# Ternary feed-forward with gathered conditioning on one core: another order for the first block

## The chip, the cores and the metric

The kernel runs on one core of a Trainium2 chip. The metric is the device time of one execution in microseconds (us), the median of three runs: 972.67 us before the change (972.66 to 973.07).

## The reference

```python
w = weights[conditions]                        # 128 samples, each a 64 x 64 matrix out of 200
u = einsum('bct,bcd->bdt', x, w)               # x: 128 x 64 x 512
# ternarize(W): delta = 0.05 * max|W|; mask = |W| > delta
#               alpha = sum(|W| where mask) / max(sum(mask), 1); Wq = alpha * sign(W) * mask
h = gelu(u @ ternarize(W1).T + b1)             # W1: 2048 x 512
y = h @ ternarize(W2).T + b2                   # W2: 512 x 2048
scale = max|y| / 7 + 1e-8
out = x + clip(round(y / scale), -7, 7) * scale
```

So each weight matrix needs its largest magnitude, then a count of the weights above the threshold and the sum of their magnitudes, before its factor alpha is known. Layer 1 may be multiplied with the plain signs before alpha is there; GELU needs alpha.

## The kernel before, in words

**Blocks.** The 128 samples go in 16 blocks of 8 (four pairs of samples, 512 columns). For each block the rows of x are mixed by the gathered matrices ("pc" products), split into a high and a low part, run through 16 chunks of layer 1 ("ph") and 16 chunks of layer 2 ("py"). Blocks 1 to 15 run in a steady order in which the two layers are interleaved two chunks apart (lines 963 to 1133). Block 0 is different, and the change lies almost wholly in it.

**Order of the work.** Every engine runs its instructions in program order: `InOrder` (line 28) wraps each engine, and line 36 is the line that all instructions carry in the profile, so groups are told apart by tile names. What each engine does next is what the Python program says next for it.

**Block 0, in order of time.**
- SP loads W1 in seven pieces, x of block 0 in two halves, b1 and W2 (lines 113 to 137). DVE takes the largest magnitudes of W1, ACT its signs and magnitudes (lines 283 to 296). PE meanwhile runs 50 products of ones ("idle", line 281) into a bank that nobody reads.
- POOL gathers four 128 x 64 tables (`fetch`, line 174, one indirect DMA for each pair) and writes each, times 64, in two 64 x 64 pieces on the diagonal of `diag` (`place`, line 186).
- The threshold: DVE's row maxima go through a transposition on PE (`thresholds`, line 229; "tops_delta_w" in the profile), then four pairs are mixed on PE (`mix0`, line 303).
- DVE makes masks (`mask1`, 128 x 2048 for each of four groups of W1) and ternary weights (`signed1`, "terns"). POOL widens one 128 x 512 chunk of them at a time to 32 bits (`widen1`, "wf<-terns", into a ring of four). A layer-1 chunk is four products with the widened weights and the high part of the mixed x, and four with the narrow weights and the low part (`layer1_0`, line 416).
- PE counts the masks (`count1`, line 339): the stationary operand is ones, a 128 x 256 piece of the mask moves, 32 products in all, into one bank "number". `alpha_1` (line 535) reduces the 256 columns on DVE; ACT sums the magnitudes (`above1`).
- Layer-1 chunks before alpha is known wait in PSUM banks (`early`, line 517, five banks in turn). `early_bend` (line 528) is then the GELU on ACT, a rounded copy on ACT, and the difference of the two: on POOL for chunks 0, 2, 4 and 6 ("h<-ring,h"), later on DVE for the others (`low`, line 468).
- DVE finds the maxima of W2 (`largest2`), its threshold (a second transposition on PE, "tops_delta_w<-ident_f,junk"), and its ternary weights (`signed2`: a comparison of 128 x 2048, "junk<-nat,minus_w", then a second instruction, "terns<-nat,delta_w,junk").
- POOL widens W2's chunks (`widen2`, a ring of four) and PE runs layer 2 of block 0 with them (lines 698 to 722); both the high and the low part of a chunk are multiplied with the widened weights. Between its chunks block 1 is mixed (`condition`, from layer-2 chunk 5 on), with tables that POOL fetched and placed at lines 613 to 638.

**Numbers that set the order:** `widen1` runs two chunks ahead of `early` (line 682); `behind(hc)` (line 662) says what DVE, ACT and POOL do after layer-1 chunk hc.

Of the kernel before, what the change touches and what calls it, by code (L numbers as in the profile page):

```python
# [8 lines left out]
F32 = mybir.dt.float32  # L9
# [7 lines left out]
ALU = mybir.AluOpType  # L17
# [3 lines left out]
P = 128  # L21
# [3 lines left out]
UP = 64.0  # L25
# [14 lines left out]
def tile_cond_ternary_ffn(  # L40
# [32 lines left out]

    const = ctx.enter_context(tc.tile_pool(name="const", bufs=1))
    big = ctx.enter_context(tc.tile_pool(name="big", bufs=20))
    gather = ctx.enter_context(tc.tile_pool(name="gather", bufs=PAIRS))
    half = ctx.enter_context(tc.tile_pool(name="half", bufs=8))
    quarter = ctx.enter_context(tc.tile_pool(name="quarter", bufs=4))
    ps_c = ctx.enter_context(tc.tile_pool(name="ps_c", bufs=2, space=PSUM))
# [84 lines left out]
    def half_of(h):  # L164
        return slice(h * C, (h + 1) * C)
# [8 lines left out]
    def fetch(n, j):  # L174

        pair = n * PAIRS + j
        wg = gather.tile([P, D], F32, tag="wg", name=f"wg_{pair}")
        pool.indirect_dma_start(
            out=wg[:, :],
            out_offset=None,  # L180
            in_=table,
            in_offset=bass.IndirectOffsetOnAxis(ap=rows[:, pair : pair + 1], axis=0),
        )
        return wg

    def place(j, wg):
        for h in range(2):
            out = diag[half_of(h), j, h * D : (h + 1) * D]
            pool.tensor_scalar(out, wg[half_of(h), :], UP, None, ALU.mult)

    def parts(n):
        return [
# [69 lines left out]
    def group1(tiles, g):  # L262
        return tiles[g // 2][:, g % 2, :]

    def sign1(g):
        act.activation(group1(signs, g), flat(nat1[g]), AF.Sign)

    def abs1(g):

        if g == NG - 1:  # L270
            mags.append(big.tile([P, GH, T], F32, tag="big", name="mag"))
        else:
            mags.append(nat1[g])
        act.activation(flat(mags[g]), flat(nat1[g]), AF.Abs)

    mags = []


    idle = ps_h.tile([P, T], F32, tag="ph", name="idle")
    pool.memset(above[:, :T], 1.0)  # L280
    for _ in range(50):
        pe.matmul(out=idle, lhsT=ones_b, rhs=above[:, :T], start=True, stop=True)
    at = 0
    for g in range(NG):
        for ks in PIECES[g]:
# [8 lines left out]
        if g < NG - 1:  # L294
            sign1(g)
            abs1(g)
    fetched = [fetch(0, j) for j in range(PAIRS)]
    for j in range(PAIRS):
        place(j, fetched[j])
    two_next = parts(0)  # L300
    pcs = []

    def mix0(j):
        pc = ps_y.tile([P, NT, P], F32, tag=f"py{j}", name=f"pc_0_{j}")
        mix(pair_of(x_next, j), j, pc)
        pcs.append(pc)

# [28 lines left out]
            ALU.mult,  # L336
        )

    def count1(g, number, first, final):
        n = number.shape[1]  # L340
        for i in range(WCH // n):
            pe.matmul(
                out=number,
                lhsT=ones_b,
                rhs=group1(masks, g)[:, i * n : (i + 1) * n],
                start=(first and i == 0),
                stop=(final and i == WCH // n - 1),
            )

    def above1(g):  # L350
# [62 lines left out]
                    stop=(c == NT - 1 and k == 1),  # L413
                )

    def layer1_0(n, hc, ph, part=slice(0, BLK), between=None):
        g, i = divmod(hc, GH)
        narrow = group1(terns, g)[:, i * T : (i + 1) * T].rearrange("p (c h) -> p c h", c=NT)
        for k in range(2):
            w = narrow if k else wide1[n, hc]  # L420
            for c in range(NT):
                if between is not None and k == 1 and c == NT - 2:
                    between()
                pe.matmul(
                    out=ph,
                    lhsT=w[:, c, :],
                    rhs=cond[n][k][:, c, part],
                    start=(c == 0 and k == 0),
                    stop=(c == NT - 1 and k == 1),
                )  # L430
# [83 lines left out]
    ring = [t[:, i, :] for t in rings for i in range(2)]  # L514
    ring += [quarter.tile([P, BLK], F32, tag="quarter", name=f"ring_{i}") for i in (10, 11)]

    def early(hc, between=None):

        slot = (hc + 1) % 5
        if slot < 2:  # L520
            ph = ps_h.tile([P, BLK], F32, tag="ph", name=f"ph_0_{hc}")
        else:
            ph = ps_y.tile([P, BLK], F32, tag=f"py{slot - 2}", name=f"ph_0_{hc}")
        for part in halves if hc == 0 else [slice(0, BLK)]:
            layer1_0(0, hc, ph[:, part], part, between)
        waiting[hc] = ph
# [8 lines left out]
    def alpha_1():  # L535

        count = const.tile([P, 1], F32, name="count1")
        dve.tensor_reduce(count, number, AX.X, ALU.add)
        dve.tensor_scalar(count, count, 1.0, None, ALU.max)
        dve.reciprocal(count, count)  # L540
        yield
        total = ps_c.tile([P, NG], F32, tag="pc", name="total1")
        pe.matmul(out=total, lhsT=ones_f, rhs=sums1, start=True, stop=True)
        kept = const.tile([P, 1], F32, name="kept1")
        dve.tensor_reduce(kept, total, AX.X, ALU.add)
        alpha[0] = const.tile([P, 1], F32, name="alpha_w1")
        dve.tensor_scalar(alpha[0], kept, count, delta1, ALU.mult, ALU.add)
        alpha[1] = without_up(0)
# [14 lines left out]
    def largest2(g):  # L563
        dve.tensor_reduce(
            top_2[:, g : g + 1], flat(nat2[g]), AX.X, ALU.max, apply_absolute_value=True
        )
# [43 lines left out]

    mask1(0, parts1[0])
    signed1(0, parts1[0])
    fetched += [fetch(1, j) for j in range(2)]
    widen1(0, 0)
    widen1(0, 1)
    fetched += [fetch(1, j) for j in range(2, PAIRS)]
    lo0(0)
    lo0(1)
    hi0(2)
# [9 lines left out]
    abs1(3)  # L629
    for g in range(NG):  # L630
        above1(g)
    number = ps_y.tile([P, T // 2], F32, tag="py3", name="number")
    count1(0, number, True, False)
    mask1(1)
    signed1(1)
    widen1(0, 4)
    for j in range(PAIRS):
        place(j, fetched[PAIRS + j])
    mask1(2)
    mask1(3)  # L640
    signed1(2)
    early(2)
    for g in range(1, NG):
        count1(g, number, False, g == NG - 1)
    find = alpha_1()
    next(find)
    early(3, lambda: next(find, None))
    widen1(0, 5)
    early(4)
    early_bend(0)  # L650
    widen1(0, 6)
    wf2 = half.tile([P, 2, T], F32R, tag="half", name="wf2")
    w2f = [wf2[:, i, :] for i in range(2)]
    w2f += [quarter.tile([P, T], F32R, tag="quarter", name=f"wf2_{i}") for i in (2, 3)]
    find = thresholds("w2", top_2, above.bitcast(F32)[:, :P])


    def ahead(hc):
        if hc == 11:
            next(find)  # L660

    def behind(hc):
        if 5 <= hc < 5 + NG:
            largest2(hc - 5)
        if hc == 7:
            sign1(3)
        if hc == 9:
            signed1(3)
        if hc == 11:
            delta.extend(next(find))  # L670
            signed2(0)
        if hc == 12:
            for i in (1, 3):
                low(0, i)
            signed2(1)
        if hc in (13, 14):
            widen2(0, hc - 13)

    for hc in range(5, NH):
        ahead(hc)  # L680
        early(hc)
        if hc + 2 < NH:
            widen1(0, hc + 2)
        early_bend(hc - 4)
        behind(hc)
    for hc in range(NH - 4, NH):
# [11 lines left out]
    for hc in range(NH - LAG):  # L698
        if hc + 2 < NH - LAG:
            widen2(0, hc + 2)  # L700
        both_layer2(0, hc)
        if hc == 0:
            signed2(2)
        if hc == 1:
            for i in range(10, NH):
                low(0, i)
        if hc < NG:
            kept(w1t, hc, terns)
        if hc == 3:
            signed2(3)  # L710
        if hc == 4:
            two_next = parts(1)
            w2t = big.tile([P, NH, T], F8, tag="big", name="w2t")
        if hc in (4, 6, 8, 9):
            g = {4: 0, 6: 1, 8: 2, 9: 3}[hc]
            count2(g)
            kept(w2t, g, terns2)
        if hc in (5, 7, 9, 11):
            j = (hc - 5) // 2
            condition(1, j, pair_of(x_next, j), two_next)  # L720
            for g in {7: [0], 9: [1], 11: [2, 3]}.get(hc, []):
                sum2(g)
    cond[1] = two_next
    x_next, two_next, fetched = [], [], []
    hf = ring[:2]
    widen1(1, 0)
    widen2(0, NH - LAG)
# [235 lines left out]
    def eight(s):  # L963
# [14 lines left out]
        if n + 1 < NB:  # L978
            if hc == 0:
                if n + 1 == SEVEN[0]:  # L980
                    extra["x"] = half.tile([P, 2, T], F32, tag="half", name="x_quarters")
                    for j in range(2):
                        quarter_x(n + 1, j)
                else:
                    x_next.append(load_x(n + 1) if n + 1 < NB - 1 else split_x(n + 1))
                two_next.append(parts7(n + 1) if n + 1 in SEVEN else parts(n + 1))
            if 2 <= hc < 2 + PAIRS:
                fetched.append(fetch(n + 1, hc - 2))
            if 7 <= hc < 7 + PAIRS:
                place(hc - 7, fetched[hc - 7 - PAIRS])  # L990
        if n == KNOWN and hc in (0, 1):
            fetch_x(order[hc])
        if n == SEVEN[0] - 1:
# [65 lines left out]
    def pair(n, k):  # L1059
# [10 lines left out]
        def behind(i):  # L1070
# [15 lines left out]
            if i == 4:  # L1086
                if not leaves:
                    widen7(ahead, 3)
                if k < PAIRS:
                    fetched.append(fetch(n + 1, k))  # L1090
                if 2 <= k < 2 + PAIRS:
                    place(k - 2, fetched[PAIRS * (n - 1) + k - 2])
                if not leaves:
                    widen7(ahead, 2)
                if parting:
# [147 lines left out]
```

## Time and profile before

| | us |
|---|---|
| median of 3 runs | 972.67 |
| the profiled execution | 972.58 |
| its span (first to last instruction) | 970.8 |
| first layer-1 product of block 0 | 20.32 |
| first layer-1 product of chunk 4 | 31.70 |
| first GELU of block 0 | 32.38 |
| first layer-2 product of block 0 | 53.89 |
| mixing of block 1 for its third pair | 74.08 |
| first layer-1 product of block 1 | 83.30 |

Times inside the execution are counted from the start of the span. PE is matrix products, PEld the loads of their stationary operands, DVE, ACT and POOL the three other compute engines, SP the engine that issues the large DMAs. In a timeline a row is one instruction or a run of like ones: start, duration of the run, engine, operation, output and inputs, shapes, count, and in brackets the idle time before it with what ended it. The records of products overlap, since they are pipelined: how far one start is from the next is what a product costs PE.

### The profile page before, as it was taken

Reading aid. Unit: us, or ns where it says so; the run is one execution under the profiler, and the core shown is the slowest. Engines: PE = TensorE matmul, PEld = TensorE weight load, DVE = VectorE, ACT = ScalarE, POOL = GpSimd, SP = SyncE. Lnnn points to the kernel's source line nnn. Section 1 sums busy time; section 2 is a strip of 40 time slices with the busy share of each in tenths; the row PEclk is TensorE's granted clock in tenths of the full one; section 3 lists DMA queues with packets and bytes.
Section 4 is the critical chain, followed back from the end, with each engine's and each line's share of the span. In section 5 each row is a group of like instructions: output and inputs, shape, how many; then the busy total and the mean of one; then the engine's idle time right before and its main releaser. Section 6 shows DMA issues by size and latency. Waiting matters only on the chain.

```text
span 970.8 us, 16879 instructions
## 1 busy us (share of the span) xinstructions
PE 960.1 (99%) x5858; PEld 727.4 (75%) x5858; DVE 659.7 (68%) x1143; ACT 613.7 (63%) x1076; POOL 662.0 (68%) x1024
## 2 busy tenths in 40 slices
PE   8999999999999999999999999999999999999996
PEld 5677667778788787887887787787887878766664
DVE  7898766666676666666666666666766765467856
ACT  7994445656656566665656666566666666467773
POOL 6877867777676676767677676776767776466541
PEclk9999999999999999999999999999999999999999
DMA  9201011010111100111110111101011111339994
GB/s 358 99 23 47 14 34 49 24 69 15 35 49 34 59 24 35 49 33 48 34 60 15 35 49 33 59 25 55 28 33 51 33 57 48 109 128 371 392 408 180
DMA packets 33158, 80.05 MB, mean 82 GB/s; under 512 B 3760, under 2 KB 3760, under 8 KB 30128
## 3 DMA queue, kind: packets, MB, share of 16 engines
q1 hardware_dynamic: 31024, 76.86, 22.0%
q0 software_dynamic: 2048, 2.10, 0.7%
q8 instruction: 47, 0.77, 0.3%
q14 instruction: 39, 0.32, 0.1%
HBM read 46.44 MB, written 32.51 MB: 81 GB/s over the span
## 4 chain that ended last, share of the span: by engine, by line
PE 97%; DVE 2%; ACT 0%; POOL 0%; issue 0%; ACTq 0%; POOLq 0%
PE py L36 46%; PE xy L36 18%; PE z L36 14%; PE ph L36 11%; PE pc L36 6%; PE idle L36 1%; DVE masks L36 1%; DVE xt L36 0%; DVE y_last L36 0%; DVE terns L36 0%; ACT diag L36 0%; PE number L36 0%; ACT ph L36 0%; DVE ymax L36 0%; DVE low_last L36 0%
## 5 line engine op out<-in xcount | busy, mean ns | idle before, releaser
L36 PE MATMUL py<-wf,h 128*128 128x512 f32 x1056 | 309.7, 418 | 0.0
L36 POOL CAST wf<-w2t 128x512 fp32r<-128x512 fp8e4 x236 | 205.6, 889 | 116.3 <-PE py L36 113.0
L36 DVE SCALAR_TENSOR_TENSOR low_parts<-ring,h 128x512 f16<-128x512 f32 x224 | 188.5, 877 | 85.9 <-ACT h L36 85.7
L36 PE MATMUL py<-w2t,low_parts 128*128 128x512 fp8e4 x944 | 228.0, 379 | 0.0
L36 PEld LDWEIGHTS py<-wf,h 128*128 128x128 f32 x1056 | 192.0, 189 | 44.8
L36 POOL CAST wf<-sums 128x256 fp32r<-128x256 fp8e4 (+1 forms) x288 | 142.1, 498 | 78.3 <-PE xy L36 75.2
L36 ACT ACTIVATE ring<-ring,b1t,alpha_up 128x512 f32<-128x512 f32 x192 | 155.9, 818 | 56.2 <-DVE ring L36 52.0
L36 DVE TENSOR_TENSOR ring<-xy,ring 128x256 f32<-128x256 f32 x192 | 106.6, 555 | 113.2 <-PE xy L36 113.2
L36 ACT COPY ring<-xy 128x256 f32<-128x256 f32 x192 | 71.6, 373 | 176.2 <-PE xy L36 175.0
L36 POOL CAST wf<-w1t 128x256 fp32r<-128x256 fp8e4 (+1 forms) x240 | 140.4, 596 | 27.8 <-PE ph L36 23.4
L36 PEld LDWEIGHTS <-low_parts 128*128 128x128 f16 x944 | 92.1, 98 | 88.8 <-issue 1.7
L36 ACT ACTIVATE h<-ring 128x512 fp32r<-128x512 f32 x224 | 130.3, 627 | 1.1
L36 POOL TENSOR_SCALAR diag<-wg 64x64 f32<-64x64 f32 x128 | 68.0, 532 | 40.0 <-DMA wg<-in_L_cond_weights,rows 36.1
L36 PEld LDWEIGHTS <-w1t 128*128 128x128 fp8e4 x768 | 63.4, 98 | 32.8 <-issue 12.8
L36 PE MATMUL xy<-xb,wf 128*128 128x256 f32 x384 | 84.7, 302 | 0.0
L36 PE MATMUL xy<-xt,wf 128*128 128x256 f32 x384 | 75.4, 277 | 0.0
L36 PE MATMUL xy<-xl,sums 128*128 128x256 f16 x384 | 75.3, 278 | 0.0
L36 POOL DMA_INDIRECT wg<-in_L_cond_weights,rows x64 | 63.0, 985 | 16.5 <-issue 13.7
L36 PE MATMUL xy<-xl,w1t 128*128 128x256 f16 x384 | 74.3, 275 | 0.0
L36 PE MATMUL ph<-x,wf 128*128 128x512 f32 (+1 forms) x260 | 73.2, 403 | 0.1
L36 PE MATMUL z<-xl,sums 128*128 128x256 f16 x384 | 73.2, 273 | 0.0
L36 ACT ACTIVATE ring<-ph,b1t,alpha_up 128x512 f32<-128x512 f32 x48 | 37.3, 777 | 54.7 <-PE ph L36 52.5
(133 smaller groups left out, 1421.8 us busy)
## 6 DMA issues: line engine op xcount, KB each, us to landing
xt<-in_x SPq DMA_DIRECT2D x38, 512.0 KB, 8.3
y_dram<-y SPq DMA_DIRECT2D x15, 1024.0 KB, 4.3
out<-xt SPq DMA_DIRECT2D x30, 512.0 KB, 8.2
x_quarters<-in_x SPq DMA_DIRECT2D x52, 256.0 KB, 2.7
nat<-in_L_ffn_W SPq DMA_DIRECT2D x6, 1024.0 KB, 10.2
y_back<-y_dram SPq DMA_DIRECT2D x2, 1024.0 KB, 10.7
nat<-in_L_ffn_W SPq DMA_DIRECT2D x3, 512.0 KB, 8.9
wg<-in_L_cond_weights,rows POOLq DMA_INDIRECT x64, 2.5
```

Of the source, the lines that this page charges most:

```text
L36: return lambda *args, **kw: self._tc.keep_in_program_order(make(*args, **kw))
```

## The change

Read in order of the file:

- The four gathered tables of a block are one tile, allocated at the first fetch. For blocks 0 and 1 they are placed by `place_all`: two instructions of 64 x (4 x 64) instead of eight of 64 x 64. Later blocks still place pair by pair.
- 46 products of ones instead of 50. The fetches of block 0 stand earlier in the program text; on POOL they are preceded by the same instructions as before.
- The mixed pairs of block 0 lie in other banks, so that layer 1 has six banks instead of five.
- A count product has a 128 x 128 piece of the mask as its stationary operand and one column of ones moving: 64 products instead of 32. The result has one column; a product with ones ("all1") adds it over the partitions, in the middle of chunk 4, where the sums of magnitudes are added too.
- Chunks 2 and 3 of layer 1 both come before the counts of groups 1 to 3; before, only chunk 2 did.
- POOL's order: chunks 0 and 1 are widened before block 1's first two fetches, chunk 5 before its last two, and chunks 6 to 8 before the first difference on POOL; from then on POOL widens three chunks ahead. Block 1's tables are placed after chunk 15 was widened, and no longer between chunks 4 and 5.
- The transposition for W2's threshold is issued in the middle of chunk 11, and no longer before it. Two of DVE's sums over W2 (`sum2`) change places with the mixing.

```diff
+        if j == 0:
+            gathered[n] = gather.tile([P, PAIRS, D], F32, tag="wg", name=f"wg_{n}")
...
+    def place_all(n):
+        for h in range(2):
+            out = diag[half_of(h), :, h * D : (h + 1) * D]
+            pool.tensor_scalar(out, gathered[n][half_of(h)], UP, None, ALU.mult)
...
-    for _ in range(50):
+    for _ in range(46):
         pe.matmul(out=idle, lhsT=ones_b, rhs=above[:, :T], start=True, stop=True)
+    for j in range(PAIRS):
+        fetch(0, j)
...
-    for j in range(PAIRS):
-        place(j, fetched[j])
+    place_all(0)
...
-        pc = ps_y.tile([P, NT, P], F32, tag=f"py{j}", name=f"pc_0_{j}")
+        home, tag = [(ps_c, "pc"), (ps_h, "ph"), (ps_y, "py0"), (ps_y, "py1")][j]
+        pc = home.tile([P, NT, P], F32, tag=tag, name=f"pc_0_{j}")
...
-        n = number.shape[1]
-        for i in range(WCH // n):
+        for i in range(WCH // P):
             pe.matmul(
                 out=number,
-                lhsT=ones_b,
-                rhs=group1(masks, g)[:, i * n : (i + 1) * n],
+                lhsT=group1(masks, g)[:, i * P : (i + 1) * P],
+                rhs=ones_b[:, :1],
...
-        slot = (hc + 1) % 5
+        slot = (hc + 4) % 6
...
-        dve.tensor_reduce(count, number, AX.X, ALU.add)
-        dve.tensor_scalar(count, count, 1.0, None, ALU.max)
+        dve.tensor_copy(count, number)
+        yield
+        all_of = ps_c.tile([P, 1], F32, tag="pc", name="all1")
+        pe.matmul(out=all_of, lhsT=ones_f, rhs=count, start=True, stop=True)
+        dve.tensor_scalar(count, all_of, 1.0, None, ALU.max)
         dve.reciprocal(count, count)
...
-    fetched += [fetch(1, j) for j in range(2)]
     widen1(0, 0)
     widen1(0, 1)
-    fetched += [fetch(1, j) for j in range(2, PAIRS)]
+    for j in range(2):
+        fetch(1, j)
...
-    number = ps_y.tile([P, T // 2], F32, tag="py3", name="number")
-    count1(0, number, True, False)
+    number = ps_c.tile([P, 1], F32, tag="pc", name="number")
+    count1(0)
+    early(2)
     mask1(1)
     signed1(1)
     widen1(0, 4)
-    for j in range(PAIRS):
-        place(j, fetched[PAIRS + j])
+    early(3)
     mask1(2)
     mask1(3)
     signed1(2)
-    early(2)
+    widen1(0, 5)
+    for j in range(2, PAIRS):
+        fetch(1, j)
+    widen1(0, 6)
     for g in range(1, NG):
-        count1(g, number, False, g == NG - 1)
+        count1(g)
     find = alpha_1()
     next(find)
-    early(3, lambda: next(find, None))
-    widen1(0, 5)
-    early(4)
+    early(4, {(1, 0): lambda: next(find), (1, 2): lambda: next(find, None)})
+    widen1(0, 7)
+    early(5)
+    widen1(0, 8)
     early_bend(0)
-    widen1(0, 6)
+    early_bend(1)
...
     def behind(hc):
-        if 5 <= hc < 5 + NG:
+        if hc == 6:
+            largest2(0)
+        if 6 <= hc < 6 + NG - 1:
             largest2(hc - 5)
...
+        if hc == 12:
+            place_all(1)
-        if hc == 9:
+        if hc == 8:
             signed1(3)
...
-    for hc in range(5, NH):
-        ahead(hc)
-        early(hc)
-        if hc + 2 < NH:
-            widen1(0, hc + 2)
+    for hc in range(6, NH):
+        early(hc, {(1, 0): lambda: next(find)} if hc == 11 else {})
+        if hc + 3 < NH:
+            widen1(0, hc + 3)
         early_bend(hc - 4)
         behind(hc)
...
-            for g in {7: [0], 9: [1], 11: [2, 3]}.get(hc, []):
+            for g in {7: [0, 1], 9: [2], 11: [3]}.get(hc, []):
                 sum2(g)
```

More of the change, by code (lines that the diff above doesn't have):

```diff
@@ L75, in tile_cond_ternary_ffn @@
     big = ctx.enter_context(tc.tile_pool(name="big", bufs=20))
-    gather = ctx.enter_context(tc.tile_pool(name="gather", bufs=PAIRS))
+    gather = ctx.enter_context(tc.tile_pool(name="gather", bufs=1))
     half = ctx.enter_context(tc.tile_pool(name="half", bufs=8))
@@ L176, in fetch @@
         pair = n * PAIRS + j
-        wg = gather.tile([P, D], F32, tag="wg", name=f"wg_{pair}")
+        if j == 0:
+            gathered[n] = gather.tile([P, PAIRS, D], F32, tag="wg", name=f"wg_{n}")
         pool.indirect_dma_start(
-            out=wg[:, :],
+            out=gathered[n][:, j, :],
             out_offset=None,
@@ L183, in fetch, with place @@
         )
-        return wg
-    def place(j, wg):
+    def place(n, j):
         for h in range(2):
             out = diag[half_of(h), j, h * D : (h + 1) * D]
-            pool.tensor_scalar(out, wg[half_of(h), :], UP, None, ALU.mult)
+            pool.tensor_scalar(out, gathered[n][half_of(h), j, :], UP, None, ALU.mult)
+    def place_all(n):
+        for h in range(2):
+            out = diag[half_of(h), :, h * D : (h + 1) * D]
+            pool.tensor_scalar(out, gathered[n][half_of(h)], UP, None, ALU.mult)
+    gathered = {}
     def parts(n):
@@ L266, in sign1 @@
         act.activation(group1(signs, g), flat(nat1[g]), AF.Sign)
+    mags = nat1[: NG - 1]
     def abs1(g):
@@ L271, in abs1 @@
             mags.append(big.tile([P, GH, T], F32, tag="big", name="mag"))
-        else:
-            mags.append(nat1[g])
         act.activation(flat(mags[g]), flat(nat1[g]), AF.Abs)
-    mags = []
     idle = ps_h.tile([P, T], F32, tag="ph", name="idle")
     pool.memset(above[:, :T], 1.0)
-    for _ in range(50):
+    for _ in range(46):
         pe.matmul(out=idle, lhsT=ones_b, rhs=above[:, :T], start=True, stop=True)
+    for j in range(PAIRS):
+        fetch(0, j)
     at = 0
@@ L296, in tile_cond_ternary_ffn @@
             abs1(g)
-    fetched = [fetch(0, j) for j in range(PAIRS)]
-    for j in range(PAIRS):
-        place(j, fetched[j])
+    place_all(0)
     two_next = parts(0)
@@ L337, in signed1, with count1 @@
         )
-    def count1(g, number, first, final):
-        n = number.shape[1]
-        for i in range(WCH // n):
+    def count1(g):
+        for i in range(WCH // P):
             pe.matmul(
                 out=number,
-                lhsT=ones_b,
-                rhs=group1(masks, g)[:, i * n : (i + 1) * n],
-                start=(first and i == 0),
-                stop=(final and i == WCH // n - 1),
+                lhsT=group1(masks, g)[:, i * P : (i + 1) * P],
+                rhs=ones_b[:, :1],
+                start=(g == 0 and i == 0),
+                stop=(g == NG - 1 and i == WCH // P - 1),
+                skip_group_check=True,
             )
@@ L414, in layer1, with layer1_0 @@
                 )
-    def layer1_0(n, hc, ph, part=slice(0, BLK), between=None):
+    def layer1_0(n, hc, ph, part=slice(0, BLK), between={}):
         g, i = divmod(hc, GH)
@@ L421, in layer1_0 @@
             for c in range(NT):
-                if between is not None and k == 1 and c == NT - 2:
-                    between()
+                between.get((k, c), lambda: None)()
                 pe.matmul(
@@ L515, in tile_cond_ternary_ffn, with early @@
     ring += [quarter.tile([P, BLK], F32, tag="quarter", name=f"ring_{i}") for i in (10, 11)]
-    def early(hc, between=None):
-        slot = (hc + 1) % 5
+    def early(hc, between={}):
+        slot = (hc + 4) % 6
         if slot < 2:
@@ L655, in tile_cond_ternary_ffn @@
     find = thresholds("w2", top_2, above.bitcast(F32)[:, :P])
-    def ahead(hc):
-        if hc == 11:
-            next(find)
     def behind(hc):
-        if 5 <= hc < 5 + NG:
+        if hc == 6:
+            largest2(0)
+        if 6 <= hc < 6 + NG - 1:
             largest2(hc - 5)
@@ L720, in tile_cond_ternary_ffn @@
             condition(1, j, pair_of(x_next, j), two_next)
-            for g in {7: [0], 9: [1], 11: [2, 3]}.get(hc, []):
+            for g in {7: [0, 1], 9: [2], 11: [3]}.get(hc, []):
                 sum2(g)
     cond[1] = two_next
-    x_next, two_next, fetched = [], [], []
+    x_next, two_next = [], []
     hf = ring[:2]
@@ L987, in eight @@
             if 2 <= hc < 2 + PAIRS:
-                fetched.append(fetch(n + 1, hc - 2))
+                fetch(n + 1, hc - 2)
             if 7 <= hc < 7 + PAIRS:
-                place(hc - 7, fetched[hc - 7 - PAIRS])
+                place(n + 1, hc - 7)
         if n == KNOWN and hc in (0, 1):
@@ L1089, in behind @@
                 if k < PAIRS:
-                    fetched.append(fetch(n + 1, k))
+                    fetch(n + 1, k)
                 if 2 <= k < 2 + PAIRS:
-                    place(k - 2, fetched[PAIRS * (n - 1) + k - 2])
+                    place(n + 1, k - 2)
                 if not leaves:
```

## The prediction

> **What bounds the kernel.** The page first, then the chain of waits, then the timelines of PE, PEld, POOL and DVE for the first 85 us.
>
> ```profile
> span 970.8 us, 16879 instructions
> ...
> PE 97%; DVE 2%; ACT 0%; POOL 0%; issue 0%; ACTq 0%; POOLq 0%
> ```
>
> PE carries 97% of the chain, so what PE saves anywhere reaches the end, unless PE later meets a wait that was hidden. The chain over the first 140 us shows where PE was not the one:
>
> ```profile
> 2.96 13.62 PE idle L36 x50
> 16.58 0.11 PE tops_delta_w L36
> 16.69 3.59 PE pc L36 x32
> ...
> 25.92 3.11 DVE masks L36 x2
> 29.03 0.04 issue
> 29.07 1.03 PE number L36 x8
> 30.10 1.38 PE ph L36 x6
> 31.48 0.12 PE total L36 x2
> 31.60 13.50 PE ph L36 x58
> ```
>
> Until 31.6 PE waits at times for DVE's masks, and the products of ones hold the transposition up; after it, it is PE alone. The counting and the late weights, in PE's and in PEld's timeline:
>
> ```profile
> 24.07 1.04 PE L36 MATMUL number<-masks,ones_b 128*128 128x256 bf16 x8
> 26.80 1.91 PE L36 MATMUL number<-masks,ones_b 128*128 128x256 bf16 x16
> 29.07 1.03 PE L36 MATMUL number<-masks,ones_b 128*128 128x256 bf16 x8 [0.36 <-DVE masks L36]
> ```
>
> ```profile
> 33.71 0.77 PEld L36 LDWEIGHTS ph<-x,wf 128*128 128x128 f32 x4 [0.36 <-POOL wf L36]
> 35.79 0.76 PEld L36 LDWEIGHTS ph<-x,wf 128*128 128x128 f32 x4 [0.48 <-POOL wf L36]
> ```
>
> **The change on PE, part by part** (first products, before and after).
>
> Start. The maxima are spread on DVE by 15.94 (copy at 15.71, 0.23), but the transposition starts at 16.42 behind 50 idle products. Four fewer at 0.216 (distance of the warm ones) end 0.86 earlier, so DVE's copy decides: with its weight load it ends about 0.3 earlier. `diag` is in time: POOL waited 3.85 for the gathers until 14.08, and two instructions from there end by 15.4 to 16.3, if each takes between 0.36 (the 64x64) and 1.1 (a 64x64 beside a busy DVE); I take 0.5. Mixing ends 0.3 earlier. Chunk 0 stood 0.33 after the last mixing product because POOL widened after a fetch (19.65 to 20.24); widened first, it is ready by 19.1. Chunk 0 starts at 19.8 instead of 20.32. Chunk 1, with 0.05 for the last low part on DVE: 21.7 instead of 22.19.
>
> Chunk 2. Its weights come from POOL, whose conversion takes 0.61 alone but 1.56 to 1.6 beside DVE's masks. The mask at 23.09 moves to 22.78 with DVE, and the conversion ends 0.47 after it again: chunk 2 at 24.57 instead of 24.89. Chunk 3 follows at 26.48 (1.91 as before), and ends at 28.28.
>
> Counting. Before: 32 products 0.109 apart = 3.49, plus 0.52 for the last mask. After: 64 products with a stationary operand each. No row shows such a stream. From below: two narrow stationary operands were loaded 15 ns apart (PEld at 20.89, two in 0.12 though one takes 0.10). From above: the "pc" products, each with its own wide operand, 0.112 apart. The nearest row is "total", four moving columns: its two products start 29 ns apart. I take 29: 16 products are 0.46, and end before chunk 2's weights; 48 are 1.39, so chunk 4 starts at 29.67. The masks of group 3 (DVE, 28.7 after the shift) are in time. The Trainium skill, "TensorE: Matmul & The Clock Gate", section "Back-to-back issue gap", speaks against the change: a sustained stream of load and product pairs is given there as about 81 ns each for 128 moving columns, and no run here shows what one column does to that. By 81 instead of 29 the 48 products would take 2.5 more, an estimate from that page, and the forecast below would be about 975.3.
>
> Chunk 4 starts at 29.67 instead of 31.70, with "all1" and "total" inside it, 0.14 each (what "total" adds between 31.10 and 31.46). Chunk 5 at 31.73 instead of 33.71; chunk 6 at 33.54 instead of 35.79, because the two waits on POOL above (about 0.2 and 0.3) go: block 1's tables are no longer placed at 27.91 to 33. At 1.807 a chunk (37.52, 39.33, 41.13) chunk 11 starts at 42.57 and layer 2 could start at 51.75 instead of 53.89: **PE is 2.14 ahead.**
>
> **What does not move.** Alpha needs the end of the counting and of chunk 4's first part: its sum is read at about 31.57, before 31.63. So ACT, which runs GELU after GELU from 32.38 to 54 and conversions to 79, and DVE, whose maxima of W2 fill 32.21 to 41.07, are only 0.06 earlier. W2's threshold is the exception: its transposition is free by 43.35 (DVE) and PE reaches it at 43.66, not 44.94.
>
> **The stretch that decides** is POOL beside DVE, from 44 to 56:
>
> ```profile
> 44.41 1.28 POOL L36 TENSOR_TENSOR h<-ring,h 128x512 fp32r<-128x512 f32 x1
> 45.63 11.99 POOL L36 CAST wf<-terns 128x512 fp32r<-128x512 bf16 x8
> ```
>
> ```profile
> 45.95 1.38 DVE L36 TENSOR_SCALAR junk<-nat,minus_w 128x2048 bf16<-128x2048 f32 x1
> 47.36 2.58 DVE L36 SCALAR_TENSOR_TENSOR terns<-nat,delta_w,junk 128x2048 bf16<-128x2048 f32 x1
> 49.87 2.11 DVE L36 TENSOR_TENSOR h<-ring,h 128x512 fp32r<-128x512 f32 x2
> 51.90 1.63 DVE L36 TENSOR_SCALAR junk<-nat,minus_w 128x2048 bf16<-128x2048 f32 x1
> 53.56 2.58 DVE L36 SCALAR_TENSOR_TENSOR terns<-nat,delta_w,junk 128x2048 bf16<-128x2048 f32 x1
> ```
>
> Eight conversions take 11.99 there, 1.5 each, where one alone takes 0.61. Seen one by one, POOL and DVE take turns: a POOL instruction that comes during one of these DVE instructions ends about 0.47 after it (47.33 and 47.80, 49.94 and 50.42, 53.53 and 53.99, 56.14 and 56.61), and DVE's copy at 42.37 took 1.04 instead of 0.23 while POOL worked. Before, the conversions for layer-1 chunks 14 and 15 paired with the first two of these DVE rows, and those for layer-2 chunks 0 and 1 with the two differences: ready at 51.4 and 52.4, 2.4 and 3.3 ahead of their use at 53.89 and 55.73. That cover hid POOL.
>
> After the change two placing instructions stand between. Before its threshold is there DVE idles; POOL's difference for chunk 6 starts at 44.35 (as before, 0.06 earlier), DVE's first comparison wants to start at 44.68 and has to let it end, at 45.57. The comparison ends 1.14 later (as 46.19 to 47.33), at 46.71; only 0.6 of the 1.3 that DVE had gained is left. From there, with the distances of the old rows: 2.62 for the long instruction (beside chunk 15's conversion), 1.02 and 1.02 for the two differences (beside the two placings, less about 0.1 because these are shorter), 1.55 for the second comparison (beside layer-2 chunk 0, ready at 53.4), 2.61 for the second long one, and 0.47: layer-2 chunk 1 is ready at 55.9. Layer-2 chunk 0 thus waits 1.65 of the 2.14, and **chunk 1 starts at 55.9 instead of 55.73**. Chunk 2's conversion takes 1.0 more and is ahead of its use at 57.7; from there POOL keeps up (1.0 against 1.81).
>
> Sum at that point: -0.3 (start), -0.2 (chunk 0), -1.5 (3.49 - 0.46 - 1.39 - 0.14), -0.5 (mask wait), -0.5 (two waits on POOL) and about 0.8 back for chunk 2's weights, which hid the counting before it, and the odd tenths: -2.14; then +2.34 of waiting on POOL: **+0.2**.
>
> **The rest, at nothing.** Six banks: chunk 10 needs GELU 4 (read by 40.3) at 40.8. The mixing of block 1 keeps its place in PE's order, and ACT, which frees it, has 3 us. `sum2` fills the 2.87 that DVE idled at 76.3; without that it costs nothing either, as alpha of W2 is wanted at 88.7 and its sums end at 87.87 or earlier. The one tile for four gathers could make placing wait for a later fetch (2.5 to land); x's two halves are slices of one tile too, and PE mixed the first pair at 16.53 though the second half, issued at 6.10, takes some 10.9 to land. SP's queue is not touched. POOL's fetches of block 1 move behind conversions (1.28 each) and end at 31.8, before chunk 6's weights are wanted at 33.5.
>
> Profiled execution 972.58 + 0.2 = **972.8** (its median of runs is 0.09 higher). Chance 0.63, its own range 971.4 to 974.0.
>
> **Rivals.**
> 1. *PE's lead survives.* If POOL finishes chunk 14's conversion before DVE's first comparison, or the placings fit beside one DVE instruction, the two layer-2 conversions pair one row earlier (53.3 for chunk 1) and wait little. Then 2.14 or most of it stays: 970.4 to 971.4. For it: DVE idled 1.83 before its threshold. Against it: PE brings that threshold 1.3 earlier. 0.17, of which 0.12 lies beyond 0.2%.
> 2. *POOL is one turn later: slower.* If DVE's comparison gets in before POOL's difference for chunk 6 (the two are 0.33 apart by my sum; it decides if DVE comes first), chunk 14 pairs with the first long DVE instruction (ready at 49.9 where PE wants it at 48.1) and layer-2 chunk 0 with the second one: 56.05 instead of 53.89, +2.2, 974.8. 0.13.
> 3. *The counting is slow.* Each ns above 29 costs 48 ns in alpha, and DVE, ACT and POOL follow it: from 65 ns on it is over +1.95; at 112 it is +4, 976.8. 0.07.
>
> **Numbers.** 0.2% is 1.95 us, about what a measurement of this kernel can tell from no change. Faster 0.12, same 0.69, slower 0.19. The range reaches from rival 1 to a little beyond rival 2: 970.4 to 975.0; what is left out is the slow end of rival 3 and a bit of each tail.
>
> **What would show it.** The 48 counting products end 1.4 after chunk 3, chunk 4 starts at 29.7, the first GELU at 32.3; a wait of PE on POOL's "wf" at the first two layer-2 chunks, of 1.6 and 0.7; layer 2's second chunk at 55.9. If PE runs through from 29 to 83 without a wait, rival 1 holds; if it waits for weights at chunk 14 of layer 1, rival 2; if the counting takes 3 us or more, rival 3.

## The result, and the profile after

The changed kernel takes 975.22 us (median of 13 runs, 973.47 to 975.62) where the kernel before takes 972.67 (13 runs of the same series, 972.54 to 973.07): a ratio of 1.0022, interval 1.0014 to 1.0031. It is 2.55 us, 0.26%, slower; that is 2.4 above the forecast and 0.2 above the upper end of its range, and by the prediction's own mark of 0.2% it is the outcome "slower", to which it gave 0.19. Of the 13 executions three lie at 973.5 to 973.7, with a mean granted clock of PE of 0.998, and ten at 975.1 to 975.6, with 0.995 to 0.997; the profiled one (975.22, span 973.4) is of the second group, and what may make the two is told below.

From the page and from the chain of waits over the first 140 us:

```profile
span 973.4 us, 16929 instructions
...
PE 95%; DVE 2%; POOL 1%; DMA 1%; ACT 0%; issue 0%; SPq 0%; POOLq 0%; ACTq 0%
```

```profile
24.36 3.88 PE ph L36 x16
28.24 1.18 PE number L36 x48
29.42 1.04 PE ph L36 x4
...
31.15 12.23 PE ph L36 x54
43.97 1.28 POOL h L36
45.25 4.17 POOL wf L36 x2
49.42 1.26 POOL diag L36
...
50.75 1.93 POOL diag L36
...
52.74 2.11 POOL wf L36
...
54.89 12.81 PE py L36 x48
```

Before, the chain was PE alone from 31.6 on. Now it leaves PE at 43.4 and runs for 11 us over POOL: its difference, the conversions of layer-1 chunks 14 and 15, the two placings ("diag"), the conversion for the first chunk of layer 2. The three timelines of that stretch, PE, POOL and DVE:

```profile
49.47 1.21 PE L36 MATMUL ph<-x,wf 128*128 128x512 f32 x4
50.53 1.04 PE L36 MATMUL ph<-x,terns 128*128 128x512 f16 x4
54.89 7.37 PE L36 MATMUL py<-wf,h 128*128 128x512 f32 x24 [3.33 <-POOL wf L36]
```

```profile
43.97 1.28 POOL L36 TENSOR_TENSOR h<-ring,h 128x512 fp32r<-128x512 f32 x1
45.20 4.22 POOL L36 CAST wf<-terns 128x512 fp32r<-128x512 bf16 x2
49.40 3.27 POOL L36 TENSOR_SCALAR diag<-wg 64x256 f32<-64x256 f32 x2
52.74 5.14 POOL L36 CAST wf<-terns 128x512 fp32r<-128x512 bf16 x4
```

```profile
44.21 2.12 DVE L36 TENSOR_SCALAR junk<-nat,minus_w 128x2048 bf16<-128x2048 f32 x1
46.37 2.58 DVE L36 SCALAR_TENSOR_TENSOR terns<-nat,delta_w,junk 128x2048 bf16<-128x2048 f32 x1
48.87 1.89 DVE L36 TENSOR_TENSOR h<-ring,h 128x512 fp32r<-128x512 f32 x2
50.69 1.27 DVE L36 TENSOR_SCALAR junk<-nat,minus_w 128x2048 bf16<-128x2048 f32 x1
52.00 2.37 DVE L36 SCALAR_TENSOR_TENSOR terns<-nat,delta_w,junk 128x2048 bf16<-128x2048 f32 x1
```

PE finishes layer 1 early (chunk 15 starts at 49.47, 2.61 earlier than before) and then stands for 3.33 us. Layer 2 begins at 54.89 instead of 53.89: **+1.0**. (The 3.33 are counted from the modelled end of the last layer-1 product, at 51.56; the next product could have started at about 51.2, as e1 and e5 show, so the wait costs 3.7.) But 24 products later the kernel is 2.5 late, though PE waits for nothing more. The table of windows says why (the columns are the window's length, then PE, PEld, DVE, ACT and POOL busy with counts, the granted clock, the DMA share and GB/s):

```profile
52.00:54.00 2.00, 0.00 (x0) 0.00 (x0) 2.00 (x1) 1.97 (x4) 1.93 (x2) 1.00 0.00 0
54.00:55.00 1.00, 0.11 (x1) 0.11 (x2) 1.00 (x2) 0.97 (x2) 1.00 (x2) 1.00 0.00 0
55.00:56.00 1.00, 1.00 (x4) 0.82 (x5) 1.00 (x2) 1.00 (x2) 1.00 (x2) 0.74 0.00 0
56.00:57.00 1.00, 1.00 (x4) 0.81 (x3) 1.00 (x2) 1.00 (x2) 1.00 (x2) 0.50 0.60 160
57.00:58.00 1.00, 1.00 (x4) 0.72 (x4) 1.00 (x2) 1.00 (x1) 0.88 (x1) 0.50 0.94 289
58.00:59.00 1.00, 1.00 (x4) 0.81 (x3) 1.00 (x2) 1.00 (x2) 0.61 (x1) 0.55 0.20 76
59.00:60.00 1.00, 1.00 (x6) 0.81 (x5) 1.00 (x1) 1.00 (x1) 0.00 (x0) 1.00 0.00 0
```

From 55 on PE is busy in all of these, but the granted clock is 0.5 from 55.48 to 58.89, 3.41 us, and products are 0.427 apart there instead of 0.227. Half of 3.41 is 1.7. The start of the ninth recorded product of layer 2 is 2.05 later than before, that of the 17th 2.52, and from there the difference stays within 2.52 and 2.54 to the end of layer 2 of the last block. So the whole result was made between 44 and 59 us: **about 2.7 of lead on PE, 3.7 of waiting for POOL, 1.6 of halved clock**; 0.1 comes back with the second product of layer 2, here and in e2. The three executions at 973.5 may be those that kept the full clock: they are 1.7 shorter. None of them has a trace.

### The profile page after: what moved, and what is told of

Same layout as the page of the kernel before. It is cut to its first block, busy times and chain, and to the rows that moved or that the text cites. A ratio compares the mean times of both kernels' runs of the same rounds, so it can differ in the third digit from the quotient of the medians.

```text
span 973.4 us, 16929 instructions
## 1 busy us (share of the span) xinstructions
PE 958.8 (99%) x5888; PEld 727.2 (75%) x5888; DVE 660.5 (68%) x1143; ACT 613.4 (63%) x1076; POOL 657.0 (67%) x1012
## 4 chain that ended last, share of the span: by engine, by line
PE 95%; DVE 2%; POOL 1%; DMA 1%; ACT 0%; issue 0%; SPq 0%; POOLq 0%; ACTq 0%
PE py L36 46%; PE xy L36 18%; PE z L36 13%; PE ph L36 11%; PE pc L36 6%; POOL wf L36 1%; DVE top L36 1%; DMA nat<-in_L_ffn_W 1%; DVE xt L36 0%; POOL diag L36 0%; DVE y_last L36 0%; ACT diag L36 0%; POOL h L36 0%; PE number L36 0%; SPq L36 0%
## 5 line engine op out<-in xcount | busy, mean ns | idle before, releaser
L36 POOL CAST wf<-w1t 128x256 fp32r<-128x256 fp8e4 (+1 forms) x240 | 138.2, 587 | 28.3 <-PE ph L36 23.5
L36 POOL TENSOR_SCALAR diag<-wg 64x64 f32<-64x64 f32 (+1 forms) x116 | 66.1, 570 | 39.4 <-DMA wg<-in_L_cond_weights,rows 36.2
L36 PEld LDWEIGHTS xy<-xt,wf 128*128 128x128 f32 x384 | 65.3, 188 | 8.6
```

Source lines behind the costliest of these rows:

```text
L36: return lambda *args, **kw: self._tc.keep_in_program_order(make(*args, **kw))
```

## The experiments

Two series, each with its own runs of the kernel before: 972.64 (series of e1 to e4) and 972.69 (e5 to e8).

**e1: place the tables of block 1 earlier.** The changed kernel with the two placings after the conversion of chunk 8, where DVE is at the maxima of W2, instead of after chunk 15's.

```diff
     widen1(0, 8)
+    place_all(1)
...
-        if hc == 12:
-            place_all(1)
```

> The changed kernel with one edit: block 1's tables are placed right after chunk 8 was widened (about 33.8, where DVE takes maxima), not after chunk 15. Theory (POOL's turns): the two placings beside DVE from 49.4 to 52.7 are what makes layer 2's first weights late. Without them the conversions for layer-2 chunks 0 and 1 pair with DVE's two differences, ready by about 50.4 and 51.4; PE starts layer 2 at 51.3 to 51.5 instead of 54.89, waits less than 0.3, and never sees a half clock: 970.2, 2.4 below the kernel before. Rival (another part of the change makes those weights late, the order three chunks ahead or the later transposition): layer 2 still starts after 53.5 and the time stays at 972 or above.

Measured 972.0 (971.84 to 972.26), ratio 0.9994 (0.9985 to 1.0003). The timelines of its POOL, its PE and, at the end, its DVE:

```profile
33.86 1.79 POOL L36 TENSOR_SCALAR diag<-wg 64x256 f32<-64x256 f32 x2
```

```profile
50.58 1.04 PE L36 MATMUL ph<-x,terns 128*128 128x512 f16 x4
51.26 11.27 PE L36 MATMUL py<-wf,h 128*128 128x512 f32 x48
...
73.22 1.16 PE L36 MATMUL pc<-diag,xt 128*128 128x128 f32 x8 [1.62 <-DVE x L36]
```

```profile
70.21 2.35 DVE L36 SCALAR_TENSOR_TENSOR terns<-nat,delta_w,junk 128x2048 bf16<-128x2048 f32 x1
72.48 1.28 DVE L36 TENSOR_TENSOR x<-pc,x 128x512 f16<-128x512 f32 x2
```

The two placings take 1.79 there, no wait stands before layer 2, the clock stays at 1.00, and the lead of 2.64 is whole up to layer-2 chunk 9. So the placings at 49.4 made both the wait and the halved clock: without them the kernel is 2.64 early there and not 2.52 late. But 1.9 of the lead is lost again at 73.22, where the mixing of block 1's third pair waits for a bank that DVE's low part of the first pair has to leave (72.48, behind the ternary weights at 70.21). That is a second bound, behind the one removed, and 3.2 us of the 5.2 reach the end. The start of layer 2 came as the theory expected (51.3 to 51.5) and not as the rival did (after 53.5). The total of 972.0 is not the 970.2 of the theory; it stands at the edge of the rival's 972, but for another reason, the new wait.

**e2: keep PE at work through the wait.** The changed kernel and 54 products of ones into a free bank, between the layers.

```diff
+    warm = ps_c.tile([P, T], F32, tag="pc", name="warm")
+    for _ in range(54):
+        pe.matmul(
+            out=warm[:, :P], lhsT=ones_b, rhs=ones_b, start=True, stop=True
+        )
```

> The changed kernel with 54 products of ones (128 columns, into a bank that nobody reads) between layer 1 and layer 2 of block 0, some 3.0 us of work in a gap of 3.33. Theory: the gap itself costs 1.0 and the half clock that follows it (3.41 us at 0.5) another 1.5 to 1.7; with PE busy the half clock goes and layer 2 starts at 54.9 as before: 973.5 in every execution, granted clock 1.00 throughout. Rival (the clock is a symptom of the waiting and the second chunk is late for want of weights): 975.2 as in the changed kernel.

Measured 974.28 (973.83 to 974.8), ratio 1.0016 (1.0007 to 1.0025).

```profile
51.37 3.18 PE L36 MATMUL warm<-ones_b 128*128 128x128 bf16 x54
54.87 7.33 PE L36 MATMUL py<-wf,h 128*128 128x512 f32 x31 [0.33 <-POOL wf L36]
```

Layer 2 starts at the same time (54.87), the clock stays at 1.00 through it, and the kernel is 0.88 late at the 17th recorded product and until about 400 us, where the changed one is 2.52 late: the halved clock cost 1.64. So the theory was right about the clock, but the total fell by 0.94 only, and not to 973.5. In the profiled run 0.4 more is lost at about 400 us and 0.55 at about 815, each time where POOL waits for a gather of tables to land; why those landings were later in this run is open.

**e3: the kernel before with the placings put late.** Block 1's tables, gathered into one tile, placed by two instructions after chunk 15's conversion, and nothing else of the change.

```diff
...
-    for j in range(PAIRS):
-        place(j, fetched[PAIRS + j])
...
+        if hc == 13:
+            place_all(1)
         if hc in (13, 14):
             widen2(0, hc - 13)
```

> The kernel before with one part of the change: the four gathered tables of a block are one tile and block 1's are placed by two instructions after chunk 15 was widened, no longer between chunks 4 and 5. Theory: this alone is the loss. The waits on POOL at chunks 5 and 6 go (0.4 gained), then chunk 15's conversion ends at 50.4, the placings take until about 53.7, and layer-2 chunk 0 is converted beside DVE's second long instruction, ready at 56.6 where PE wants it at 53.5: 975.3 if the clock stays, 977.0 if the gap of 3 halves it. Rival (the placing is only late because of what else was put ahead of it): 972.0 to 972.7.

Measured 974.58 (974.35 to 974.84), ratio 1.002 (1.0011 to 1.0029): slower by 1.9, on its own. Its PE and POOL:

```profile
55.79 6.46 PE L36 MATMUL py<-wf,h 128*128 128x512 f32 x27 [1.65 <-POOL wf L36]
```

```profile
50.29 3.27 POOL L36 TENSOR_SCALAR diag<-wg 64x256 f32<-64x256 f32 x2
```

Layer 2 starts at 55.79 instead of 53.89 after an idle time of 1.65, without a halved clock: the sign was as expected, the size less than the 975.3. POOL's two placings take 3.27 here too. Of the 0.4 that was to come back at chunks 5 and 6, chunk 5 starts 0.3 earlier than in the kernel before, but chunk 6 only 0.1: its conversion still stands behind POOL's first difference.

**e4: the kernel before with the new counting alone.**

```diff
...
-                lhsT=ones_b,
-                rhs=group1(masks, g)[:, i * n : (i + 1) * n],
+                lhsT=group1(masks, g)[:, i * P : (i + 1) * P],
+                rhs=ones_b[:, :1],
...
```

> The kernel before with the new counting alone: masks as stationary operands, one column of ones moving, 64 products, and the sum over the partitions inside chunk 3. Theory: the products come 25 ns apart, as in the changed kernel, but the counting of groups 1 to 3 follows chunk 2 and waits for group 3's mask at 29.0, so only 0.4 for the last group is won and 0.14 paid for the added sum: 972.4. Rival (the products saved, 3.49 less 1.60 less 0.14, all reach the end): 970.9.

Measured 972.64 (972.26 to 975.09), ratio 1.0005 (0.9996 to 1.0014): inconclusive by time, as five of the eleven executions lie at 973.4 to 975.1 with a lower mean clock (0.994 to 0.997), and none of these has a trace; what slowed them is open. In the profiled one (972.42, where 972.4 was expected) the difference is a constant -0.19 in block 0.

```profile
29.14 0.55 PE L36 MATMUL number<-ones_b,masks 128*128 128x1 bf16 x16 [1.00 <-DVE masks L36]
```

Alone, the faster counting runs into the next wait for masks (and the chunks behind it into one for weights).

**e5: e1 without the second bound.** The changed kernel with e1's edit, and two more: the third and fourth pair of block 1 are mixed into the banks of layer 1, which are free by then, and DVE's third sum over W2 goes behind the last low part.

```diff
...
-            condition(1, j, pair_of(x_next, j), two_next)
-            for g in {7: [0, 1], 9: [2], 11: [3]}.get(hc, []):
+            condition(1, j, pair_of(x_next, j), two_next, (ps_h, "ph") if j > 1 else (ps_c, "pc"))
+            for g in {7: [0, 1], 11: [2, 3]}.get(hc, []):
                 sum2(g)
```

> The changed kernel with block 1's tables placed early (as in e1_place_early), block 1's third and fourth pair mixed into the two banks of layer 1 that are free then, and W2's third sum put behind the last low part. Theory: in e1_place_early PE's lead of 2.64 was lost at 71.6 to 73.2 because the mixing of the third pair waits for a bank that DVE frees after 8 us of other work; with a bank of its own PE does not wait, and the last low part comes before layer 1 of block 1 asks for it: the lead of 2.6 reaches the end, 970.0. Rival (the next bound is DVE or ACT itself, which have not moved by more than 0.5): PE waits for the low or high part of block 1 instead and the time is 971.5 or more.

Measured **970.02** (969.96 to 970.85), ratio 0.9974 (0.9963 to 0.9985), as expected (970.0): 2.7 under the kernel before and 5.2 under the changed one. The timeline shows no wait of PE from 30 to 88 us, and the lead of 2.7 is there at the end.

**e6: e5 with that sum where the change put it,** ahead of the last low part. Only the banks differ from e1.

> The same without moving W2's third sum. Theory: the third sum (2.3 on DVE) stands between the third and the fourth low part, so the fourth ends at about 82.1 where PE asks for it at 81.6: 0.5 is lost there, 970.5. Rival (the order of the sums does not matter once the bank is there): the same as e5_banks_and_sums.

Measured 971.08 (971.01 to 971.72), ratio 0.9984 (0.9975 to 0.9993).

```profile
80.42 1.07 PE L36 MATMUL ph<-x,wf 128*128 128x512 f32 x4
82.35 1.02 PE L36 MATMUL ph<-x,w1t 128*128 128x512 f16 x4 [0.86 <-DVE x L36]
```

```profile
81.31 1.04 PE L36 MATMUL ph<-x,w1t 128*128 128x512 f16 x4
```

Layer 1 of block 1 waits for the fourth low part on DVE: 1.0 of the lead goes, twice what was expected. In e5 (the second view) the same products start at 81.31, with no wait.

**e7: e5 with the old counting** (32 products of 256 columns with ones as the stationary operand).

> e5_banks_and_sums with the old counting: ones as stationary operand, 32 products of 256 columns, the reduction over columns on DVE. Theory: now nothing covers the counting, so its price is paid in full: 48 products at 25 ns and 0.14 for the added sum become 24 at 109 (2.6 instead of 1.35), and PE, alpha and all that follows come 1.2 to 1.4 later: 971.3. Rival (as in e4_before_new_count, where the same edit moved the profiled execution by 0.2): within 0.3 of e5_banks_and_sums.

Measured 971.18 (971.14 to 971.45), ratio 0.9985 (0.9976 to 0.9994): 1.16 more than e5. The PE timelines of e7 and of e5:

```profile
28.02 2.78 PE L36 MATMUL number<-masks,ones_b 128*128 128x256 bf16 x24
30.55 1.17 PE L36 MATMUL ph<-x,wf 128*128 128x512 f32 x4
```

```profile
28.06 1.34 PE L36 MATMUL number<-ones_b,masks 128*128 128x1 bf16 x48
29.26 1.17 PE L36 MATMUL ph<-x,wf 128*128 128x512 f32 x4
```

Chunk 4 starts 1.29 later with the old counting, and the end is 1.16 later, as the theory expected (971.3): nothing hides it any more. The same edit was worth 0.2 in e4.

**e8: e5 with the placings after the first two conversions for layer 2,** again beside DVE's ternary weights of W2.

```diff
...
-    place_all(1)
...
         if hc in (13, 14):
             widen2(0, hc - 13)
+        if hc == 14:
+            place_all(1)
```

> e5_banks_and_sums with the placing back beside DVE, but behind the conversions for layer-2 chunks 0 and 1. Theory (turns): those two conversions now pair with DVE's two differences and are ready by 51.5, the placings take the turns of the second comparison and part of the second long instruction, and the conversion for chunk 2 is ready at about 54.8 to 55.3 where PE wants it at 55.1: 970.0 to 970.4. Rival (any placing beside DVE costs its 3.3 us whatever stands before it): PE waits 1 us or more at chunk 2, 971 or more.

Measured 972.03 (971.85 to 972.16), ratio 0.9993 (0.9984 to 1.0002): 2.0 more than e5. Its POOL, DVE and PE:

```profile
51.64 4.21 POOL L36 TENSOR_SCALAR diag<-wg 64x256 f32<-64x256 f32 x2
55.92 9.89 POOL L36 CAST wf<-terns 128x512 fp32r<-128x512 bf16 x8
```

```profile
51.11 1.63 DVE L36 TENSOR_SCALAR junk<-nat,minus_w 128x2048 bf16<-128x2048 f32 x1
52.78 2.36 DVE L36 SCALAR_TENSOR_TENSOR terns<-nat,delta_w,junk 128x2048 bf16<-128x2048 f32 x1
```

```profile
51.41 4.02 PE L36 MATMUL py<-wf,h 128*128 128x512 f32 x16
57.07 7.59 PE L36 MATMUL py<-wf,h 128*128 128x512 f32 x32 [1.64 <-POOL wf L36]
```

The rival's outcome came: chunks 0 and 1 of layer 2 are on time, and chunk 2 waits 1.64. The first placing ends 0.7 after DVE's comparison (53.45 against 52.74), the second 0.7 after the long instruction (55.85 against 55.14): 4.2 for what takes 1.79 at 33.86 in e1. The sum had met these two instructions, but had let the second placing end part of the way through the long one.

## Why the prediction was wrong in size, by its own steps

- **PE's lead: right, and a little small.** Chunk 0 at 19.66 (forecast 19.8), chunk 1 at 21.66 (21.7), chunk 2 at 24.36 (24.57), chunk 4 at 29.28 (29.67), chunk 11 at 42.09 (42.57), first GELU at 31.93 (32.3). Layer 2 could have started at about 51.2, as in e1 (51.26) and e5 (51.18), instead of 51.75: 2.7 ahead and not 2.14. One reason given was half of it: that the waits on POOL at chunks 5 and 6 go because block 1's tables are no longer placed before them. In e3, which moves only these, chunk 6 still starts 2.29 after chunk 5, against 1.81 in the changed kernel, which also widens further ahead.
- **Counting: right.** The 48 products take 1.20 from 28.08 to 29.28, 25.0 ns each (forecast 29, bounds 15 and 112). The section "Wait — 56ns, not 53.3ns?" of the Trainium skill's page "TensorE: Matmul & The Clock Gate" gives about 25 ns as the least distance of two products, however few the columns; the runs agree, here with a new stationary operand for each. The 81 ns for 128 columns that the prediction quoted from the same page did not come; that the 975.3 worked out from them lies near the measured 975.22 is chance.
- **Who comes first at 44: right.** POOL's difference (43.97) came before DVE's first comparison (44.21), which ended 1.08 after that difference did (1.14 by the forecast) and took 2.12. So rival 2's condition did not occur.
- **The placings: the step that failed.** The prediction took 0.5 for each and set the two beside the two differences, "1.02 and 1.02 ... less about 0.1". Beside DVE's maxima, which do not hold it up, one takes 0.85 to 0.86 (two take 1.78 at 14.08, 1.79 in e1). In the stretch that decides, the first began in the first difference (48.87 to 49.96), ended 0.71 after it and lasted 1.28, through nearly the whole second difference; the second placing began 0.07 after DVE's second comparison (50.69 to 51.96) and ended 0.71 after that, at 52.67, after 1.92. So the conversion for layer-2 chunk 0, set beside that comparison, fell beside the next long instruction (52.00 to 54.37) and took 2.11 instead of 1.55. By terms: chunk 15's conversion ended at 49.42 and not 49.80 (-0.4), the placings with the gaps between took 3.3 instead of 2.04 (+1.3), the conversion +0.56: ready at 54.84 instead of 53.4, 1.45 later. PE's wait at this chunk, 1.65 by the forecast, grew by these 1.45 and by the 0.55 of additional lead: 3.65. The bounds given at the start (0.36 to 1.1 for one) hold the 0.85 but not the 1.28 and 1.92; the turns were counted from the middle value only, and one more turn costs a whole DVE instruction. The second wait of the forecast, 0.7 at layer-2 chunk 1, did not come: its weights were ready at 55.85 (forecast 55.9), but chunk 0 was so late that PE would not have asked for them before about 56.7.
- **The halved clock: not foreseen.** The prediction costed PE's waits at their length. The one at 51.56 lasted 3.33 and brought 3.41 at half clock behind it, 1.64 by e2 against the changed kernel. That is the rest of the difference: without it the profiled execution would be about 0.9 late, as e2 is at that place. From the forecast's +0.2 to the measured +2.5: -0.55 (more lead), +2.0 (chunk 0), -0.7 (chunk 1), +1.6 (clock), -0.1 (second product).
- **"The mixing of block 1 keeps its place in PE's order, and ACT, which frees it, has 3 us": wrong,** and hidden in the changed kernel, whose PE was late. DVE's low part is what frees that bank last. In e1 it cost 1.9; e6 shows that the banks give back 0.9 of it, and e5 that the place of `sum2` gives the other 1.1. Rival 1's 970.4 to 971.4 therefore needed more than the lead to survive; with both it is 970.0.
- **Rival 2's price came without its condition.** It was +2.2 for POOL one turn later, if DVE came first. POOL came first and lost the turn at the placings: +1.0 at layer 2, and the clock.

Not settled: why three of 13 executions of the changed kernel are 1.7 shorter. That they kept the full clock is argued from their time and mean clock alone. A possible reason stands in the clock records of the traces: between its first rise and its later changes there lie whole multiples of 3.413 us in every profiled run (14 from the rise at 7.69 to the fall at 55.48 in the changed kernel; 280 to 282 up to the last fall in the others), and that first rise lies anywhere from 6.8 to 8.7 us after the start of the span. The step that ended with the fall at 55.48 held 2.83 of the 3.33 us of waiting; where the steps lie otherwise, the same wait is divided otherwise between two of them. No run here tests that.

## What to carry to other kernels

When an engine gets early, ask which other engine now has to serve it in the same stretch, and count the turns in which POOL and DVE hold each other up for both ends of an unknown duration: here a small POOL instruction that met a DVE comparison or long instruction cost the rest of that instruction and most of its own time. Work of no urgency on POOL goes where DVE does what does not hold POOL up, such as the maxima in e1. A wait of PE is not worth its length alone: near 3.3 us it took half as much again through the clock, and a repaired wait should be followed along PE for the next one, since the gain of 2.7 was only there after three repairs (e1, then both of e5).

## What the runs showed of the hardware

- **PE's clock after a wait.** An idle time of 3.33 us of PE was followed by 3.41 us at a granted clock of 0.5, beginning 0.6 after PE was at work again; idle times of 1.65 (e3) and 1.64 (e8) by none; with 54 products of ones in the wait there was none either (e2). The Trainium skill, "TensorE: Matmul & The Clock Gate", section "What's actually happening", gives about 3.4 us of idleness for the half clock and as long at work for its release; the length agrees with the 3.41 here. The wait was a little shorter than that, though, and PE had worked again for 0.6 us when the clock fell: here less than 3.4 us of idleness was enough.
- **POOL beside DVE.** A placing of 64x256 takes 0.85 to 0.86 beside DVE's maxima (14.08 in the changed kernel, 33.86 in e1). Where it meets a DVE difference, comparison or long instruction, it ends 0.71 after the end of that instruction (six times, in the changed kernel, e3 and e8). DVE is held up too: a difference takes 0.68 with POOL idle (59.13 in the kernel before), 1.09 beside conversions and 0.88 beside a placing (49.89 in the changed kernel, 55.07 in e8). The Trainium skill, "SBUF — State Buffer", section "Who interferes with whom", says that a DVE instruction with two inputs in SBUF contends with a POOL instruction that reads there: the difference and the long instruction, which have two, agree. For an instruction with one tensor input, as the comparison, the section names contention in DVE's two-port modes alone, and no run here shows which mode it ran in. Why a placing holds a difference up by 0.2 only, though 0.7 of the placing is still to run, is open.
- **Narrow products.** Products of one column with a fresh 128x128 stationary operand each follow one another every 25.0 ns (48 in 1.20 us, in the changed kernel).
